# A two-layer graph network on one core: who gathers the source rows, and how many instructions make the messages

## The chip, the cores and the metric

The kernel runs on one NeuronCore of a Trainium2 chip. That core has five engines with instruction queues of their own: TensorE (PE, matrix products, with a weight load PEld that overlaps them), VectorE (DVE), ScalarE (ACT), GpSimd (POOL) and SyncE (SP). SP, ACT and POOL also issue DMA transfers. PE and the transposing and element-wise instructions here meet in PSUM, the accumulators' memory; everything else lies in SBUF. The metric is the device time of one execution in microseconds. A profiled execution gives the busy time of each engine, who waited for whom, and the clock that was granted to PE.

## What is computed

Two message-passing layers over the same graph of 6250 nodes and 200000 edges, each followed by a residual and a layer norm. A node has 160 features: 64 scalars and 32 vectors of three components. Every edge has a source `src`, a target `dst` (sorted), four attributes (one scalar e0, one vector e1) and ten radial features. Cut to what matters:

```python
# layer 0: messages are products of the source row with the edge's attributes
ss, vv = s[src], v[src]
dot  = einsum('eui,ei->eu', vv, e1)
out0 = C0 * (ss * e0 @ W1 + dot * INV3 @ W2)
out1 = C1 * (p3 + p4 + p5)                     # products of ss, vv, e0, e1 with W3, W4, W5
m_agg = segment_sum(concat(out0, out1), dst)
x1 = layernorm(x + (x + relu(m_agg @ Ws_Wv)))

# layer 1: a small network of the radial features weights the source row (the factor node_vec1 of a node is left out here)
h = relu(edge_attr_10 @ W_fc1 / sqrt(10)) * sqrt(2)
w0, w1, w2, w3 = split(h @ W_fc2 / sqrt(100))   # 64, 64, 32, 32 columns
y0, y1 = l0[src], l1[src]                       # rows of x1 @ W_l1
m0 = w0 * y0 * e0
m1 = (w1 * y0)[:, :, None] * e1[:, None, :]
m2 = (w2 * e0)[:, :, None] * y1
m3 = w3 * einsum('eud,ed->eu', y1, e1) * INV3
out = layernorm(x1 + (x1 @ W_si + 0.5 * segment_sums(m0..m3, dst) @ W_l2))
```

## The kernel before

The sorted edges are cut into 391 chunks (`NCH`) of 512 edges; a chunk is four tiles (`J`) of 128 edges. A chunk's targets fall into a narrow window of nodes, at most 32 wide; the first 312 chunks (`HALF`) have one window each, the last 79 have two, one for each half of the partitions. `ORDER` mixes the two kinds, eight of the first and then up to four of the second, and `POS` is a chunk's place in it.

A layer (`sums`, L355) is a software pipeline: a loop over steps t runs a list of stages, each with a lag, on the chunk whose turn it is (L656 to L667). The order of instructions on every engine is the order of that loop, since the schedule is manual.

- `load` gathers the source rows of a chunk, one indirect DMA on POOL for each tile of 128 rows (`gathered`, L245, L247). The table is `x` in layer 0 and `ytab`, the transformed rows, in layer 1. The buffers `g` are a ring of eight chunks (`GRING`), shared by both layers; the first three chunks go to `early` before anything else runs. In layer 1 it also loads the radial features; in both, now and then, the attributes of 32 chunks.
- `onehot` makes, for every edge, its one-hot row in the window, times each of the four attributes (L457, L461, VectorE); `S` is a ring of three.
- In layer 1 `hidden` makes the first part of the radial network: for every second chunk two products into one PSUM tile `ph` (L470), and for every chunk one ReLU on ScalarE into `h` (L473). `message` then does half a chunk at a time: two products into a PSUM tile `pw` of two tiles (L483, two buffers), and three multiplications of the gathered rows with it on VectorE (L486, L491 twice). So a chunk takes six VectorE instructions.
- `matmuls` multiplies the one-hot tiles with the gathered rows (layer 0) or the messages (layer 1), and adds up in a PSUM tile `ab` for each window (L503): four blocks of 32 partitions, one for each attribute.
- `add` transposes 32x32 blocks of `ab` on VectorE into the free columns of the same tile (L524 in layer 1, L526 in layer 0) and adds the result to `acc` at the window's place (L528). In layer 1 the sums of attribute 0 are needed from the first half of the columns, those of the others from the second; `joined` therefore copies attribute 0's block first, 32 partitions by 160 columns, with ScalarE (L510), over the second half, and VectorE transposes that half alone.

When the last chunk that touches a block of 128 nodes is through, the block is closed by a second list of steps: in layer 0 a projection (L547), ReLU, residual, layer norm, a turn (L597), a linear map (L611, L612), and the rows of `ytab` and `btab` are written (L540, L623). Layer 1 cannot gather before all of `ytab` is in DRAM. In layer 1 a block is projected into a part of the tile `bank` (L634), gets its residual (L639) and norm, and is sent. At step 8 (`PREPARE`) of layer 0 the weights are loaded on SP's queue and scaled on VectorE (`prepare`, L286; L350 scales `wc`).

In layer 0 POOL has two helpers. In every run of 16 places (`EVERY`), the fourth tile of two chunks isn't gathered by POOL: the source numbers of that tile are loaded into one partition (L377), and SP (for the last place of the 16) or ScalarE (for the eighth) reads eight of them a step into registers (L395) and starts eight plain row copies (L399) into a tile `row`. When the chunk comes, ScalarE copies `row` to the fourth tile of `g` (`place_rows`, L404). That begins with the chunk at place 15 and holds for 47 chunks.

Of the kernel before, what the change touches and what calls it, by code (L numbers as in the profile page):

```python
# [10 lines left out]
F32 = mybir.dt.float32  # L11
BF16 = mybir.dt.bfloat16
I32 = mybir.dt.int32
AF = mybir.ActivationFunctionType
ALU = mybir.AluOpType
# [33 lines left out]


EVERY = 16
ROWS = P // EVERY
# [68 lines left out]
def gnn_kernel(ctx: ExitStack, tc: tile.TileContext, x, src, dst, ea, sh, avec,  # L121
# [117 lines left out]
    with tc.If(go > 0) as both:  # L239
        windowed(tc, x, srcs, src, rel, low, ident, iota, early, ahead, ea, sh, avec, *weights, out)  # L240
# [4 lines left out]
def gathered(nc, g, srcs, table, c, tiles=J):  # L245
    for j in range(tiles):
# [6 lines left out]
def windowed(ctx: ExitStack, tc: tile.TileContext, x, srcs, src, rel, low, ident, iota, early, ahead, ea, sh, avec,  # L253
# [24 lines left out]
    wn2 = const.tile([M1, 2 * D], F32, name="wn2")  # L278
# [76 lines left out]
    def sums(layer, table, gp, hp):  # L355
        with ExitStack() as s:
# [5 lines left out]
            rp = s.enter_context(tc.tile_pool(name=f"r{layer}", bufs=2))  # L362
            pa = s.enter_context(tc.tile_pool(name=f"pa{layer}", bufs=3 if layer else 4, space=PSUM))
            if layer:
                ph_ = s.enter_context(tc.tile_pool(name="ph", bufs=1, space=PSUM))
                pp = s.enter_context(tc.tile_pool(name="pp", bufs=2, space=PSUM))
            s.enter_context(tc.manual_schedule())
            G, S, SH, ET, H, M, PA, AT, RAW, NUM, ROW = ({} for _ in range(11))


            helpers = {} if layer else {EVERY - 1: (nc.sync, mybir.EngineType.SP),
                                       EVERY // 2 - 1: (nc.scalar, mybir.EngineType.Activation)}
            helped = {ORDER[i] for i in range(EVERY // 2, NCH) if i % EVERY in helpers}

            def numbers(c):
                NUM[c] = rp.tile([1, P], I32, name=f"num{POS[c] % EVERY}")
                nc.sync.dma_start(NUM[c], src[:, c, J - 1:J].rearrange("p a -> a p"))  # L377

            def fetch_rows(c):
                i = POS[c]  # L380
                for place, (queue, engine) in helpers.items():

                    k = (i - place - 1) % EVERY
                    due = i - k + EVERY - 1
                    if due >= NCH or ORDER[due] not in helped:
                        continue
                    d = ORDER[due]
                    if d not in NUM:
                        numbers(d)
                    if d not in ROW:  # L390
                        ROW[d] = rp.tile([P, D], F32, name=f"row{place}")
# [670 lines left out]
```

## Time and profile before

| | |
|---|---|
| median of 14 runs | 3905.62 us (3904.21 to 3907.64) |
| the profiled execution | 3905.87 us |
| its span | 3904.0 us |
| busy: PE / DVE / ACT / POOL | 3077.5 / 2027.8 / 492.0 / 2916.6 us |
| share of the span | 79% / 52% / 13% / 75% |
| mean granted clock of PE | 0.802 |
| moved by DMA | 296.88 MB, 76 GB/s |

The 40 slices of the page, 97.6 us each, show two stages, with the layers' border near the middle of the twentieth:

```profile
PE   3345677777777777766788899899999999999998
...
DVE  4223323333333334344466666666666767777776
ACT  2000000000000000001111111111111111111111
POOL 7777777777777777777577777777777777777776
PEclk7666655555655565667799999999999999999999
```

A digit is the busy share in tenths; PEclk is the granted clock of PE. The groups that follow are costly lines of the page, as line, engine, operation, output and inputs, count, busy time, mean of one in nanoseconds, and the idle time just before them:

```profile
L503 PE MATMUL ab<-m,S 128*128 128x320 f32 (+1 forms) x3760 | 958.5, 445 | 4.4 <-DVE acc L528 3.5
L483 PE MATMUL pw<-fc,h 100*128 100x192 f32 x3128 | 662.0, 343 | 159.4 <-DVE m L491 80.6
...
L486 DVE TENSOR_TENSOR m<-pw,g 128x256 f32<-128x256 f32 x782 | 330.7, 423 | 523.5 <-DMA g<-ytab,srcs 434.0
...
L491 DVE TENSOR_TENSOR m<-g,pw 128x192 f32<-128x192 f32 x1564 | 476.5, 346 | 0.0
...
L510 ACT ACTIVATE ab<-ab 32x160 f32<-32x160 f32 x470 | 121.3, 265 | 1353.5 <-PE ab L503 1138.3
L473 ACT ACTIVATE h<-ph 100x512 f32<-100x512 f32 x391 | 228.3, 584 | 208.1 <-PE ph L470 204.1
...
L524 DVE STREAM_TRANSPOSE ab<-ab 128x160 f32<-128x160 f32 x470 | 167.5, 356 | 13.6 <-issue 8.8
```

PE shows two instructions for each product of this data type. 470 is the number of windows, 1564 that of tiles.

### The profile page before, as it was taken

How to read it: one execution, taken by the hardware profiler on the slowest of the kernel's cores; microseconds unless marked ns; L12 is line 12 of the kernel's file. 1: busy time of each engine (PE TensorE's matmuls, PEld its weight loads, DVE VectorE, ACT ScalarE, POOL GpSimd, SP SyncE). 2: the span in 40 equal slices, each digit the busy share in tenths (PEclk: the TensorE clock that was granted, in tenths of full speed). 3: DMA queues.
4: the chain of work that ended last, by engine and by line, in shares of the span. 5: the costliest groups of instructions: out<-in, count | busy, mean ns of one | idle time of the engine just before them, and what ended most of it. 6: DMA issues, size and time to landing. Idle time of an engine off the chain costs nothing.

```text
span 3904.0 us, 61514 instructions
## 1 busy us (share of the span) xinstructions
PE 3077.5 (79%) x12754; PEld 2112.2 (54%) x12755; DVE 2027.8 (52%) x6485; ACT 492.0 (13%) x1264; POOL 2916.6 (75%) x3086
## 2 busy tenths in 40 slices
PE   3345677777777777766788899899999999999998
PEld 3234444454445555544555566566666666666666
DVE  4223323333333334344466666666666767777776
ACT  2000000000000000001111111111111111111111
POOL 7777777777777777777577777777777777777776
PEclk7666655555655565667799999999999999999999
DMA  3323333333333333333223332333333333333332
GB/s 83 74 69 73 73 76 73 75 74 81 76 77 76 79 77 82 77 82 85 67 73 73 74 74 71 75 74 76 74 80 76 77 77 77 75 81 75 81 77 69
DMA packets 215130, 296.88 MB, mean 76 GB/s; under 512 B 71494, under 2 KB 158156, under 8 KB 214746
## 3 DMA queue, kind: packets, MB, share of 16 engines
q0 software_dynamic: 147888, 252.59, 27.0%
q1 hardware_dynamic: 53782, 33.56, 3.1%
q10 hardware_dynamic: 13076, 6.70, 0.7%
q8 instruction: 107, 1.75, 0.2%
q14 instruction: 277, 2.27, 0.2%
HBM read 280.60 MB, written 12.00 MB: 75 GB/s over the span
## 4 chain that ended last, share of the span: by engine, by line
POOL 23%; issue 21%; DMA 21%; PE 16%; DVE 9%; ACTq 5%; SPq 5%; ACT 1%; DVEq 0%; POOLq 0%
POOL g L247 23%; DMA g<-ytab,srcs 10%; PE ab L503 8%; DMA g<-in_x,srcs 7%; ACTq L399 4%; SPq L399 3%; DVE m L491 3%; DMA row<-in_x 3%; PE pw L483 3%; DVE m L486 2%; PE ph L547 1%; ACTq L395 1%; SPq L395 1%; PE ph L470 1%; DVE ab L524 1%
## 5 line engine op out<-in xcount | busy, mean ns | idle before, releaser
L247 POOL DMA_INDIRECT g<-ytab,srcs x1564 | 1479.5, 946 | 500.1 <-issue 397.6
L247 POOL DMA_INDIRECT g<-in_x,srcs x1505 | 1425.1, 947 | 462.1 <-issue 403.4
L503 PE MATMUL ab<-g,S 128*128 128x160 f32 (+1 forms) x3736 | 1019.0, 459 | 562.9 <-DMA g<-in_x,srcs 298.0
L503 PEld LDWEIGHTS ab<-g,S 128*128 128x128 f32 (+1 forms) x3736 | 695.3, 278 | 893.2 <-DMA g<-in_x,srcs 478.1
L503 PE MATMUL ab<-m,S 128*128 128x320 f32 (+1 forms) x3760 | 958.5, 445 | 4.4 <-DVE acc L528 3.5
L483 PE MATMUL pw<-fc,h 100*128 100x192 f32 x3128 | 662.0, 343 | 159.4 <-DVE m L491 80.6
L483 PEld LDWEIGHTS pw<-fc,h 100*128 100x128 f32 x3128 | 504.1, 191 | 424.5 <-issue 306.5
L503 PEld LDWEIGHTS ab<-m,S 128*128 128x128 f32 (+1 forms) x3760 | 612.4, 193 | 219.8 <-issue 44.4
L486 DVE TENSOR_TENSOR m<-pw,g 128x256 f32<-128x256 f32 x782 | 330.7, 423 | 523.5 <-DMA g<-ytab,srcs 434.0
L526 DVE STREAM_TRANSPOSE ab<-ab 128x160 f32<-128x160 f32 x470 | 169.5, 361 | 647.6 <-PE ab L503 643.4
L491 DVE TENSOR_TENSOR m<-g,pw 128x192 f32<-128x192 f32 x1564 | 476.5, 346 | 0.0
L461 DVE TENSOR_TENSOR S<-bank,sh 128x384 f32<-128x384 f32 (+2 forms) x782 | 431.6, 552 | 61.9 <-PE ab L503 11.7
L528 DVE TENSOR_TENSOR acc<-acc,ab 128x120 f32 (+2 forms) x940 | 261.4, 278 | 216.7 <-ACT acc L584 143.0
L510 ACT ACTIVATE ab<-ab 32x160 f32<-32x160 f32 x470 | 121.3, 265 | 1353.5 <-PE ab L503 1138.3
L473 ACT ACTIVATE h<-ph 100x512 f32<-100x512 f32 x391 | 228.3, 584 | 208.1 <-PE ph L470 204.1
L457 DVE TENSOR_TENSOR bank<-ramp,rel 128x96 f32<-128x96 f32 (+2 forms) x782 | 200.9, 257 | 18.1 <-PE bank L634 17.7
L524 DVE STREAM_TRANSPOSE ab<-ab 128x160 f32<-128x160 f32 x470 | 167.5, 356 | 13.6 <-issue 8.8
L621 DVE SCALAR_TENSOR_TENSOR base<-pl,a_sb,z 128x160 f32<-128x160 f32 (+1 forms) x49 | 18.8, 384 | 281.5 <-ACT y L618 257.0
L547 PE MATMUL ph<-w_or_et,acc 128*128 128x160 f32 (+1 forms) x490 | 130.9, 446 | 5.5 <-DVE acc L528 5.0
L547 PEld LDWEIGHTS ph<-w_or_et,acc 128*128 128x128 f32 (+1 forms) x490 | 122.2, 312 | 15.9 <-issue 6.7
L470 PE MATMUL ph<-early,fc 10*100 10x512 f32 x392 | 110.9, 632 | 2.3 <-DMA early<-in_ea 2.3
L470 PE MATMUL ph<-w_or_et,fc 10*100 10x512 f32 x390 | 109.1, 628 | 3.0 <-DMA w_or_et<-in_ea 2.9
(95 smaller groups left out, 820.1 us busy)
## 6 DMA issues: line engine op xcount, KB each, us to landing
row<-in_x SPq DMA_DIRECT2D x3072, 0.6 KB
row<-in_x ACTq DMA_DIRECT2D x2944, 0.6 KB
g<-ytab,srcs POOLq DMA_INDIRECT x1564
g<-in_x,srcs POOLq DMA_INDIRECT x1505
raw<-in_sh SPq DMA_DIRECT2D x88, 64.0 KB
early<-in_ea SPq DMA_DIRECT2D x98, 40.0 KB
xt<-in_x SPq DMA_DIRECT2D x48, 80.0 KB
ytab<-y ACTq DMA_DIRECT2D x48, 80.0 KB
```

The lines of the kernel that those rows point to most:

```text
L247: nc.gpsimd.indirect_dma_start(out=g[:, j, :], out_offset=None, in_=table, in_offset=bass.IndirectOffsetOnAxis(ap=srcs[:, c, j:j + 1], axi ...
L399: queue.dma_start(ROW[d][a + n:a + n + 1, :], table[ds(at[n], 1), :])
L461: nc.vector.tensor_tensor(S[c][:, :, :, :w], oh[:, :, None, :w].to_broadcast([P, J, 4, w]), attr[:, :, :, None].to_broadcast([P, J, 4, w]) ...
L470: nc.tensor.matmul(ph[:, i, :], fc1[g:g + 10, :], ET[c // 4][g:g + 10, c % 4 // 2, :], start=True, stop=True)
L473: nc.scalar.activation(H[c], H["p"][:, c % 2, :].rearrange("f (p j) -> f j p", j=J), AF.Relu, scale=FC_SCALE)
L483: nc.tensor.matmul(pw[:, j, :], h[:, q + j, :], fc2, start=True, stop=True)
L486: nc.vector.tensor_tensor(mq[:, :, :, 0:64], pw[:, :, 0:128].rearrange("p j (a u) -> p j a u", a=2), y[:, :, None, 0:64].to_broadcast([P, ...
L491: nc.vector.tensor_tensor(mq[:, :, a, 64:160].rearrange("p j (d u) -> p j d u", d=3), y1, pw[:, :, None, w:w + 32].to_broadcast([P, 2, 3, ...
L503: nc.tensor.matmul(ab[:, :n], one[h * i:h * i + h, j, :, :], t[h * i:h * i + h, j, :], start=(j == 0), stop=(j == J - 1), skip_group_check ...
L524: nc.vector.transpose(tr, blocks[:, 1])
L528: nc.vector.tensor_tensor(v, v, tr[:, :, :width(c)], op=ALU.add)
L547: nc.tensor.matmul(po[:r], lhs, weights[:, g, :], start=(g == 0), stop=(g == 4))
```

## The change

The helpers of layer 0 go: `numbers`, `fetch_rows` and `place_rows` with their stages and pools, and `gathered` always takes all four tiles. In layer 1 `hidden` makes one activation for the two chunks that share `ph`. `message` takes a chunk at a time: `pw` becomes one tile of four times 256 columns (192 used) with a single buffer in place of two tiles of two, and each of the three multiplications covers the whole chunk. `joined` goes; `add` transposes the second half of `ab` for all partitions and then the first half for partitions 0 to 31, over the first result. The last residual `z` moves into the space of the weights `wn2`, which layer 1 doesn't use, in two slots by turns.

```diff
@@ -46,10 +46,6 @@
 
 FINAL = NCH - 25
 AHEAD = 3
-EVERY = 16
-ROWS = P // EVERY
 FOLD = 104
 
 
@@ -237,20 +233,20 @@
     go = nc.values_load(fits[0:1, 0:1], min_val=0, max_val=1,
                         skip_runtime_bounds_check_because="a comparison's result")
     with tc.If(go > 0) as both:
-        windowed(tc, x, srcs, src, rel, low, ident, iota, early, ahead, ea, sh, avec, *weights, out)
+        windowed(tc, x, srcs, rel, low, ident, iota, early, ahead, ea, sh, avec, *weights, out)
     with both.Else():
         general(tc, x, srcs, rel, dst, ea, sh, avec, *weights, out)
 
 
-def gathered(nc, g, srcs, table, c, tiles=J):
-    for j in range(tiles):
+def gathered(nc, g, srcs, table, c):
+    for j in range(J):
         nc.gpsimd.indirect_dma_start(out=g[:, j, :], out_offset=None, in_=table,
                                      in_offset=bass.IndirectOffsetOnAxis(ap=srcs[:, c, j:j + 1], axis=0))
     return g
 
 
 @with_exitstack
-def windowed(ctx: ExitStack, tc: tile.TileContext, x, srcs, src, rel, low, ident, iota, early, ahead, ea, sh, avec,
+def windowed(ctx: ExitStack, tc: tile.TileContext, x, srcs, rel, low, ident, iota, early, ahead, ea, sh, avec,
              w1t, w2t, w3t, w4t, w5t, ws, wv, wsi0, wsi1, wl10, wl11,
              w00, w10, w01, w11, wfc1, wfc2, out):
 
@@ -275,7 +271,9 @@
     w_or_et = const.tile([P, 7 * D], F32, name="w_or_et")
     wb = w_or_et[:, :5 * D].rearrange("p (g d) -> p g d", d=D)
     wn = w_or_et[:, 5 * D:]
-    wn2 = const.tile([M1, 2 * D], F32, name="wn2")
+
+    wn2_or_z = const.tile([P, 2 * D], F32, name="wn2_or_z")
+    wn2 = wn2_or_z[:M1]
     wc = const.tile([P, 5, D], F32, name="wc")
     fc1 = const.tile([P, 100], F32, name="fc1")
     fc2 = const.tile([100, 192], F32, name="fc2")
@@ -359,53 +357,16 @@
             if not layer:
                 pn = s.enter_context(tc.tile_pool(name="pn", bufs=1, space=PSUM))
                 up = s.enter_context(tc.tile_pool(name="up", bufs=1))
-            rp = s.enter_context(tc.tile_pool(name=f"r{layer}", bufs=2))
             pa = s.enter_context(tc.tile_pool(name=f"pa{layer}", bufs=3 if layer else 4, space=PSUM))
             if layer:
                 ph_ = s.enter_context(tc.tile_pool(name="ph", bufs=1, space=PSUM))
-                pp = s.enter_context(tc.tile_pool(name="pp", bufs=2, space=PSUM))
+                pp = s.enter_context(tc.tile_pool(name="pp", bufs=1, space=PSUM))
             s.enter_context(tc.manual_schedule())
-            G, S, SH, ET, H, M, PA, AT, RAW, NUM, ROW = ({} for _ in range(11))
-
-
-            helpers = {} if layer else {EVERY - 1: (nc.sync, mybir.EngineType.SP),
-                                       EVERY // 2 - 1: (nc.scalar, mybir.EngineType.Activation)}
-            helped = {ORDER[i] for i in range(EVERY // 2, NCH) if i % EVERY in helpers}
-
-            def numbers(c):
-                NUM[c] = rp.tile([1, P], I32, name=f"num{POS[c] % EVERY}")
-                nc.sync.dma_start(NUM[c], src[:, c, J - 1:J].rearrange("p a -> a p"))
-
-            def fetch_rows(c):
-                i = POS[c]
-                for place, (queue, engine) in helpers.items():
-
-                    k = (i - place - 1) % EVERY
-                    due = i - k + EVERY - 1
-                    if due >= NCH or ORDER[due] not in helped:
-                        continue
-                    d = ORDER[due]
-                    if d not in NUM:
-                        numbers(d)
-                    if d not in ROW:
-                        ROW[d] = rp.tile([P, D], F32, name=f"row{place}")
-                    if k == EVERY // 2 and due + EVERY < NCH:
-                        numbers(ORDER[due + EVERY])
-                    a = k * ROWS
-                    _, at = nc.values_load_multi_w_load_instructions(
-                        NUM[d][0:1, a:a + ROWS], engines=[engine], min_val=0, max_val=N - 1,
-                        skip_runtime_bounds_check_because="node numbers")
-                    for n in range(ROWS):
-                        queue.dma_start(ROW[d][a + n:a + n + 1, :], table[ds(at[n], 1), :])
-
-            def place_rows(c):
-                if c in helped:
-                    del NUM[c]
-                    nc.scalar.activation(G[c][:, J - 1, :], ROW.pop(c), AF.Copy)
+            G, S, SH, ET, H, M, PA, AT, RAW = {}, {}, {}, {}, {}, {}, {}, {}, {}
 
             def load(c):
                 if layer or c not in ahead:
-                    G[c] = gathered(nc, gp.tile([P, J, D], F32, name="g"), srcs, table, c, J - (c in helped))
+                    G[c] = gathered(nc, gp.tile([P, J, D], F32, name="g"), srcs, table, c)
                 else:
                     G[c] = ahead.pop(c)
                 if c % 4 == 0 and layer:
@@ -464,33 +425,35 @@
             def hidden(c):
 
                 if c % 2 == 0:
-                    ph = H["p"] = ph_.tile([100, 2, CH], F32, name="ph")
-                    for i in range(min(2, NCH - c)):
+                    n = min(2, NCH - c)
+                    ph = ph_.tile([100, 2, CH], F32, name="ph")
+                    for i in range(n):
                         g = 64 * i
                         nc.tensor.matmul(ph[:, i, :], fc1[g:g + 10, :], ET[c // 4][g:g + 10, c % 4 // 2, :],
                                          start=True, stop=True)
-                H[c] = wp.tile([100, J, P], F32, name="h")
-                nc.scalar.activation(H[c], H["p"][:, c % 2, :].rearrange("f (p j) -> f j p", j=J),
-                                     AF.Relu, scale=FC_SCALE)
+                    h = wp.tile([100, 2, J, P], F32, name="h")
+                    nc.scalar.activation(h[:, 0:n], ph[:, 0:n, :].rearrange("f i (p j) -> f i j p", j=J),
+                                         AF.Relu, scale=FC_SCALE)
+                    for i in range(n):
+                        H[c + i] = h[:, i]
 
             def message(c):
 
                 m = M[c] = wp.tile([P, J, 320], F32, name="m")
                 h = H.pop(c)
-                for q in range(0, J, 2):
-                    pw = pp.tile([P, 2, 192], F32, name="pw")
-                    for j in range(2):
-                        nc.tensor.matmul(pw[:, j, :], h[:, q + j, :], fc2, start=True, stop=True)
-                    y = G[c][:, q:q + 2, :]
-                    mq = m[:, q:q + 2, :].rearrange("p j (a u) -> p j a u", a=2)
+                pw = pp.tile([P, J, 256], F32, name="pw")
+                for j in range(J):
+                    nc.tensor.matmul(pw[:, j, 0:192], h[:, j, :], fc2, start=True, stop=True)
+                y = G[c]
+                mq = m.rearrange("p j (a u) -> p j a u", a=2)
+                nc.vector.tensor_tensor(
+                    mq[:, :, :, 0:64], pw[:, :, 0:128].rearrange("p j (a u) -> p j a u", a=2),
+                    y[:, :, None, 0:64].to_broadcast([P, J, 2, 64]), op=ALU.mult)
+                y1 = y[:, :, 64:160].rearrange("p j (d u) -> p j d u", d=3)
+                for a, w in ((0, 128), (1, 160)):
                     nc.vector.tensor_tensor(
-                        mq[:, :, :, 0:64], pw[:, :, 0:128].rearrange("p j (a u) -> p j a u", a=2),
-                        y[:, :, None, 0:64].to_broadcast([P, 2, 2, 64]), op=ALU.mult)
-                    y1 = y[:, :, 64:160].rearrange("p j (d u) -> p j d u", d=3)
-                    for a, w in ((0, 128), (1, 160)):
-                        nc.vector.tensor_tensor(
-                            mq[:, :, a, 64:160].rearrange("p j (d u) -> p j d u", d=3), y1,
-                            pw[:, :, None, w:w + 32].to_broadcast([P, 2, 3, 32]), op=ALU.mult)
+                        mq[:, :, a, 64:160].rearrange("p j (d u) -> p j d u", d=3), y1,
+                        pw[:, :, None, w:w + 32].to_broadcast([P, J, 3, 32]), op=ALU.mult)
 
             def matmuls(c):
                 one = S.pop(c)
@@ -504,11 +467,6 @@
                                          start=(j == 0), stop=(j == J - 1), skip_group_check=True)
                 del G[c]
 
-            def joined(c):
-
-                for ab in PA[c]:
-                    nc.scalar.activation(ab[0:32, D:2 * D], ab[0:32, 0:D], AF.Copy)
-
             def add(c):
                 for w, ab in zip(windows(c), PA.pop(c)):
                     if w % 8 == 0:
@@ -521,7 +479,9 @@
                     tr = ab[:, n:].rearrange("p (b f) -> p b f", f=W)
                     blocks = ab[:, :n].rearrange("p (l b f) -> p l b f", b=5, f=32)
                     if layer:
+
                         nc.vector.transpose(tr, blocks[:, 1])
+                        nc.vector.transpose(tr[0:32], blocks[0:32, 0])
                     else:
                         nc.vector.transpose(tr, blocks[:, 0])
                     v = acc[:, :, ds(AT[w // 8][w % 8], width(c))]
@@ -635,7 +595,8 @@
 
             def residual_last(b):
                 r = rows(b)
-                z = T["z", b] = np_.tile([P, D], F32, name="z")
+                turn = sorted(CLOSE, key=CLOSE.get).index(b) % 2
+                z = T["z", b] = wn2_or_z[:, D * turn:D * turn + D]
                 nc.vector.scalar_tensor_tensor(z[:r], T.pop(("po", b))[:r], a_sb[:r, b:b + 1],
                                                T.pop(("base", b))[:r], op0=ALU.mult, op1=ALU.add)
                 moments(b, z)
@@ -645,11 +606,11 @@
                 sent_rows(nc.sync, b, out[b * P:b * P + rows(b), :], T.pop(("o", b)))
 
             if layer:
-                stages = [(load, 0), (joined, 4), (onehot, 1), (hidden, 1), (add, 4), (message, 2), (matmuls, 3)]
+                stages = [(load, 0), (onehot, 1), (hidden, 1), (add, 4), (message, 2), (matmuls, 3)]
                 parts = [(fetch_base, 3, 2), (project_last, 5, 4), (residual_last, 6, 5), (deviation, 7, 5),
                          (sent, 8, 6)]
             else:
-                stages = [(fetch_rows, 0), (load, 0), (place_rows, 1), (onehot, 1), (add, 3), (matmuls, 2)]
+                stages = [(load, 0), (onehot, 1), (add, 3), (matmuls, 2)]
                 parts = [(fetch, 4, 1), (project, 6, 3), (rectify, 6, 4), (residual, 8, 4), (deviation, 9, 4),
                          (lambda b: normed("x1", b), 10, 5), (turned, 11, 5), (kept, 12, 5), (linear, 13, 7),
                          (written, 14, 7)]
```

## The prediction

> **What bounds the kernel now.** First the costliest groups of the page, then the waits of POOL, which say whether that engine ever stands still.
>
> ```profile
> L247 POOL DMA_INDIRECT g<-ytab,srcs x1564 | 1479.5, 946 | 500.1 <-issue 397.6
> L247 POOL DMA_INDIRECT g<-in_x,srcs x1505 | 1425.1, 947 | 462.1 <-issue 403.4
> ...
> POOL g L247 <- issue: 800.9, 2628, 0.3
> POOL g L247 <- PE ab L503: 49.9, 153, 3.6
> ...
> POOL g L247 <- DMA btab<-base: 23.9, 1, 23.9
> ```
>
> The share of POOL is only 75%, but the idle time is made of 0.3 us pieces: one between every two gathers, whatever the releaser is called. A gather takes 0.946 us, then 0.30 us pass, then the next one starts. Only two waits are longer, 3.6 us and 23.9 us. The timeline gives the ends of the two chains of gathers:
>
> ```profile
> 19.95 0.95 POOL L247 DMA_INDIRECT g<-in_x,srcs  x1 [0.30 <-issue]
> ...
> 1905.98 0.95 POOL L247 DMA_INDIRECT g<-in_x,srcs  x1 [0.30 <-issue]
> ...
> 1930.86 0.94 POOL L247 DMA_INDIRECT g<-ytab,srcs  x1 [23.93 <-DMA btab<-base]
> ...
> 3885.57 0.95 POOL L247 DMA_INDIRECT g<-ytab,srcs  x1 [0.30 <-issue]
> ```
>
> Layer 1: (3885.57 - 1930.86) / 1563 = 1.2506 us from one gather to the next, so both layers hang on POOL from end to end. Layer 0, without its 3.27 us of extra wait: (1905.98 - 19.95 - 3.27) / 1504 = 1.2518 us. The profiled span is thus 20.0 us of start, 1886 us of layer 0 gathers, 24.9 us of turn, 1954.7 us of layer 1 gathers and 18.4 us of end; 1.87 us lie outside it (3905.87 - 3904.0). The 14 runs have a median of 3905.62, 0.25 below this execution.
>
> The next view is the windows of the whole core. It shows the room that the other engines have:
>
> ```profile
> 1000.00:1500.00 500.00, 376.92 (x1232) 248.42 (x1232) 186.75 (x547) 35.08 (x107) 378.06 (x400) 0.59 0.32 78
> ...
> 3000.00:3500.00 500.00, 463.06 (x2118) 318.62 (x2115) 356.82 (x1120) 90.48 (x236) 378.36 (x400) 0.99 0.31 77
> ```
>
> The columns are PE, PEld, DVE, ACT and POOL busy, granted clock, DMA share and GB/s. Each has exactly 400 gathers in 500 us. In layer 1 a chunk (four gathers, 5.00 us) holds 463.06/100 = 4.63 us of PE, 3.57 us of DVE, 0.90 us of ACT. So PE has 0.37 us a chunk to spare, and that is where the change could do harm.
>
> **The gathers given back to POOL.** The two helpers fetch one tile of 128 rows each in every 16 chunks: 3072 + 2944 rows are 47 tiles (47 placing activations at L404). The order of the changed program on POOL is 12 + 1552 + 1564 gathers instead of 12 + 1505 + 1564, so 47 more, all in layer 0: 47 x 1.2506 = **+58.8 us**. Nothing hides them. All 3128 gathers together need 3128 x 1.2506 = 3912 us, more than the whole time now. What goes with the helpers, 6016 row copies on the queues of SP and ACT at 0.41 us a row, their register loads, 47 index loads and 47 activations of 336 ns, is off that path and is worth nothing by itself, except in two places.
>
> The first is the stall near the start:
>
> ```profile
> 81.95 0.62 DVE L350 TENSOR_SCALAR wc<-wc 128x800 f32<-128x800 f32 x1 [5.38 <-DMA row<-in_x]
> ...
> 84.24 8.04 PE L503 MATMUL ab<-g,S 128*128 128x160 f32 x39 [9.40 <-issue]
> ...
> 86.98 0.95 POOL L247 DMA_INDIRECT g<-in_x,srcs  x1 [3.57 <-PE ab L503]
> ```
>
> The releaser is named after a row, but what L350 reads is `wc`, whose loads stand on SP's queue behind the helper's rows; it is scaled 5.38 us late; VectorE works in order, the one-hot tiles behind that scaling are late, PE stops for 9.4 us, a gathered buffer comes free late and POOL waits 3.57 instead of 0.30. Without the rows, the 23 loads behind the memsets that end at 62.6 need some 10.5 us of issue (0.45 us each, their spacing now) and 2 us to land: about 75, before VectorE reaches L350 at 76.57. **-3.3 us**; at worst 0.
>
> The second is the turn between the layers:
>
> ```profile
> 1885.72 3.04 PE L503 MATMUL ab<-g,S 64*128 64x160 f32 x20 [5.19 <-ACT g L404]
> ```
>
> The last helped chunk holds PE until 1885.7, and PE and VectorE carry that backlog to the end: the last chunk's matmuls end near 1912.4, though its last gather ends at 1906.93 and should land about 2.66 us later (as the one at 1008.22 did), so 1910.1 with the last matmuls. **-2.0 us** of the 24.9; between -2.3 and 0.
>
> **Layer 1's messages.** Six instructions a chunk become three of double size. From 423 ns for 256 elements and 346 for 192, 1.2 ns an element and 115 fixed: 512 takes 731, 384 takes 577, so 1.89 us instead of 2.23, -135 us of VectorE over 391 chunks (bounds: nothing, and half of the six, -436). The second transpose adds at most 470 x 0.36 = 167 us (the row of L524), at least 0. VectorE ends near where it was, 3.57 + 0.08 us a chunk of 5.00. On ACT 121 us of copies go, and 391 activations of 584 ns become 196 of about 1.05 (0.9 ns an element from the 160- and 512-element rows). ACT is 18% busy there. All this is worth **0** while POOL's 5.00 us cover it.
>
> What can cost is the buffer of `pw`: one of four tiles in place of two of two. The next chunk's eight `pw` passes now wait for the third message instruction of this chunk, and the message starts when all four tiles have landed, not two. Queued behind them on PE are the scatter matmuls of the chunk, its projection and `ph`; VectorE's message and add wait for these, then the ring of eight gathered buffers, then POOL, which notices after some seven chunks (35 us) of lag. In a loop: after the scatter of chunk c-2 ends, VectorE needs 0.82 (one-hot) + two windows of 0.36 + 0.36 + 0.28 + message 1.89 = 4.71 us, PE 1.57 + 2.4 = 4.0 and in most iterations 1.0 to 1.6 more. Both are under 5.00, except where a block ends (1.4 us of VectorE more, once in eight chunks); the lag drains.
>
> **The end.** There a block closes every second chunk, and the chain of waits stays on PE without a gap:
>
> ```profile
> 3885.42 1.56 PE bank L634 x10
> 3886.98 1.30 PE pw L483 x8
> 3888.28 2.40 PE ab L503 x16
> ```
>
> For the last chunk the whole message stands in place of its second half (+0.77), two transposes are added (+0.71), two waits for ACT's copies go (-0.5), and I allow +0.5 for PE behind the single `pw`. **+1.5 us**; at least -0.9 (copies gone, transposes covered), at most +5.5 (0.4 us in each of the last ten chunks besides).
>
> **Sum.** 3904.0 + 58.8 - 3.3 - 2.0 + 1.5 = 3959.0; with 1.87 outside, **3961 us**, 55 above the median. Lower end: 3904.0 + 58.8 - 3.3 - 2.3 - 0.9, and layer 0's gathers at layer 1's distance (1552 x 0.0012 = -1.9): 3956. Upper end: no stall and no backlog saved, +5.5 at the end: 3970.
>
> **The skill against the rows.** The Trainium skill, "DMA: Bandwidth & Descriptors", section "Issuing engines are not separate DMA queues", says that starting DMAs from several engines saves only the time of the starting, usually small beside the transfer. By that, giving 47 tiles back to POOL would cost about nothing, and the sum would be 3902. This trace has the other case: the starting, 1.25 us a tile, is what POOL is made of.
>
> **Rivals.** (1) *PE becomes the bound in layer 1.* If the single `pw` leaves half a message (1.1 us before, the part once covered) uncovered on PE in each chunk, 4.63 + 1.1 = 5.73 us against 5.00: 391 x 0.73 = +285, 4246 us; it decides from 0.37 us a chunk. For it: PE's 93%, and 80.6 us of `pw` waits on the message already. Against it: the scatter of the chunk before lies between two groups of `pw`. 6%; most of its cases lie far below that price, from 3970 on.
> (2) *VectorE holds POOL up.* The longest layer 1 gather took 1020 ns, 74 over the median; one such delay for each added transpose is 470 x 0.074 = +35, 3996 us. Against it: the mean is 946 and 947 where VectorE is 37% and 71% busy. 4%.
> The skill's "SBUF — State Buffer", section "SBUF: two separate sides", has the rule that speaks against this change: VectorE in a two-port mode locks GpSimd out while it writes descriptors. If all 470 new transposes did so for their 0.36 us, it would be +169, 4130 us; the 946 and 947 above show nothing of the kind for the transposes already there.
> (3) *Faster: gathers come at a shorter distance once 6016 row copies no longer share the DMA engines.* The place is layer 0; the 1552 gathers there would need 55/1552 = 35 ns less each to break even; at twice that, 1.18 us, it ends at 3906 - 54 = 3852 us. For it: the row of 1.2518 in layer 0 against 1.2506. Against it: that is 1.2 ns, and layer 1, without any row copy, has the same 946 + 300. 3%. That the tiles don't all go to POOL is excluded by the program's order.
>
> **How the numbers follow.** The forecast has 87%, the rivals 6, 4 and 3. The range 3955 to 3970 holds nearly all of the first. A difference under 0.2% (7.8 us) counts as none: slower 0.965, within 0.2% 0.01, faster 0.025.
>
> **What would show it.** In the profile after: 1552 gathers from `in_x`, 1.25 us apart in both layers; no wait of 3.6 us on POOL near 87; first layer 1 gather near 1984 and the last near 3939; some 20 us behind that one. The forecast is wrong if gathers in layer 1 show waits over 0.3 us on the message (rival 1), or last longer than 0.95 (rival 2), or come closer together (rival 3).

## The result and the profile after

| | before | after |
|---|---|---|
| median of the runs | 3905.46 us (28 runs, 3904.17 to 3909.01) | 3963.76 us (6 runs, 3960.45 to 3966.79) |
| ratio | | 1.0148, 95% interval 1.0138 to 1.0158 |
| the profiled execution, and its span | 3905.87 and 3904.0 us | 3965.24 and 3963.5 us |

The changed kernel is 58.3 us slower by the medians and 59.5 us by the spans of the two profiles. The groups of POOL after, then two of its waits (total, times, longest):

```profile
L243 POOL DMA_INDIRECT g<-ytab,srcs x1564 | 1479.7, 946 | 497.9 <-issue 403.3
L243 POOL DMA_INDIRECT g<-in_x,srcs x1552 | 1469.4, 947 | 472.8 <-issue 398.5
...
POOL g L243 <- issue: 801.8, 2632, 0.3
...
POOL g L243 <- DMA ytab<-y: 21.7, 1, 21.7
```

1552 gathers of layer 0 in place of 1505, each as long as before, and behind the first chunks one wait alone that is longer than 0.3 us, the turn between the layers. The timeline of POOL gives the first and the last gather of each layer:

```profile
21.20 0.95 POOL L243 DMA_INDIRECT g<-in_x,srcs  x1 [0.30 <-issue]
...
1962.15 0.95 POOL L243 DMA_INDIRECT g<-in_x,srcs  x1 [0.30 <-issue]
...
1984.80 0.94 POOL L243 DMA_INDIRECT g<-ytab,srcs  x1 [21.70 <-DMA ytab<-y]
...
3939.76 0.94 POOL L243 DMA_INDIRECT g<-ytab,srcs  x1 [0.30 <-issue]
```

Set against the same four points of before, the difference of the spans falls apart like this (us):

| stage | before | after | difference | predicted |
|---|---|---|---|---|
| up to the first gather of layer 0's own chain | 19.95 | 21.20 | +1.25 | 0 |
| layer 0's gathers | 1886.03 | 1940.95 | +54.92 | +58.8 - 3.3 |
| turn | 24.88 | 22.65 | -2.23 | -2.0 |
| layer 1's gathers | 1954.71 | 1954.96 | +0.25 | 0 |
| from the last gather's start to the end | 18.43 | 23.74 | +5.3 | +1.5 |
| sum | 3904.0 | 3963.5 | +59.5 | +55.0 |

The windows of after (start and end, length, then PE, PEld, DVE, ACT and POOL busy, granted clock, DMA share, GB/s) say the same from the other engines' side:

```profile
1000.00:1500.00 500.00, 377.97 (x1177) 245.84 (x1178) 179.71 (x527) 30.38 (x91) 378.17 (x401) 0.58 0.30 74
3000.00:3500.00 500.00, 454.94 (x2088) 319.33 (x2086) 369.93 (x926) 55.29 (x65) 378.39 (x400) 0.98 0.31 77
```

400 gathers in 500 us, as before. ACT has 35 us less to do in the second window, DVE 13 us more, PE 8 us less, and none of it moves the time. What layer 1's edits did to the instructions stands in the groups of VectorE and ScalarE:

```profile
L449 DVE TENSOR_TENSOR m<-pw,g 128x512 f32<-128x512 f32 x391 | 270.5, 692 | 436.8 <-DMA g<-ytab,srcs 389.8
...
L454 DVE TENSOR_TENSOR m<-g,pw 128x384 f32<-128x384 f32 x782 | 394.5, 546 | 0.0
...
L484 DVE STREAM_TRANSPOSE ab<-ab 32x160 f32<-32x160 f32 x470 | 165.4, 352 | 16.2
...
L435 ACT ACTIVATE h<-ph 100x1024 f32<-100x1024 f32 x196 | 200.3, 1022 | 1619.9 <-PE ph L432 1616.1
```

By these rows the three message instructions are busy for 270.5 + 394.5 = 665.0 us; the six half ones were for 330.7 + 476.5 = 807.2. Two instructions in a row overlap at their border, though, and rows of different lines count that twice: taken together, VectorE's instructions that write `m` are busy for 632.2 us, and were for 739.7, so 107 us less. The second transpose costs 352 ns, although it handles a quarter of the partitions of the first (356 ns): 165 us more. VectorE thus has more to do than before, 2106.9 us in the whole instead of 2027.8.

### The profile page after: what moved, and what is told of

Same layout as the page of the kernel before. It is cut to its first block, busy times and chain, and to the rows that moved or that the text cites. A ratio compares the mean times of both kernels' runs of the same rounds, so it can differ in the third digit from the quotient of the medians.

```text
span 3963.5 us, 40347 instructions
## 1 busy us (share of the span) xinstructions
PE 3213.2 (81%) x12754; PEld 2157.6 (54%) x12755; DVE 2106.9 (53%) x5782; ACT 342.0 (9%) x552; POOL 2961.4 (75%) x3133
## 4 chain that ended last, share of the span: by engine, by line
POOL 30%; issue 22%; DMA 22%; PE 15%; DVE 10%; ACT 1%; DVEq 0%; ACTq 0%; POOLq 0%
POOL g L243 30%; DMA g<-in_x,srcs 13%; DMA g<-ytab,srcs 9%; PE ab L466 8%; DVE m L454 3%; DVE m L449 2%; PE ph L507 2%; PE pw L446 2%; DVE S L422 2%; DVE ab L483 1%; PE pl L572 1%; DVE ab L484 1%; PE pl L571 1%; ACT acc L282 1%; DVE bank L418 1%
## 5 line engine op out<-in xcount | busy, mean ns | idle before, releaser
L243 POOL DMA_INDIRECT g<-in_x,srcs x1552 | 1469.4, 947 | 472.8 <-issue 398.5
L466 PE MATMUL ab<-g,S 128*128 128x160 f32 (+1 forms) x3736 | 1173.9, 493 | 508.4 <-DMA g<-in_x,srcs 398.7
L466 PEld LDWEIGHTS ab<-g,S 128*128 128x128 f32 (+1 forms) x3736 | 726.6, 288 | 965.1 <-DMA g<-in_x,srcs 675.3
L446 PE MATMUL pw<-fc,h 100*128 100x192 f32 x3128 | 613.1, 340 | 196.8 <-DVE m L454 96.9
L449 DVE TENSOR_TENSOR m<-pw,g 128x512 f32<-128x512 f32 x391 | 270.5, 692 | 436.8 <-DMA g<-ytab,srcs 389.8
L454 DVE TENSOR_TENSOR m<-g,pw 128x384 f32<-128x384 f32 x782 | 394.5, 546 | 0.0
L435 ACT ACTIVATE h<-ph 100x1024 f32<-100x1024 f32 x196 | 200.3, 1022 | 1619.9 <-PE ph L432 1616.1
L484 DVE STREAM_TRANSPOSE ab<-ab 32x160 f32<-32x160 f32 x470 | 165.4, 352 | 16.2
L543 ACT ACTIVATE rl<-ph 128x160 f32<-128x160 f32 (+1 forms) x49 | 14.9, 304 | 931.6 <-PE ph L507 931.0
```

The source lines that it names most:

```text
L243: nc.gpsimd.indirect_dma_start(out=g[:, j, :], out_offset=None, in_=table, in_offset=bass.IndirectOffsetOnAxis(ap=srcs[:, c, j:j + 1], axi ...
L446: nc.tensor.matmul(pw[:, j, 0:192], h[:, j, :], fc2, start=True, stop=True)
L449: nc.vector.tensor_tensor(mq[:, :, :, 0:64], pw[:, :, 0:128].rearrange("p j (a u) -> p j a u", a=2), y[:, :, None, 0:64].to_broadcast([P, ...
L454: nc.vector.tensor_tensor(mq[:, :, a, 64:160].rearrange("p j (d u) -> p j d u", d=3), y1, pw[:, :, None, w:w + 32].to_broadcast([P, J, 3, ...
L466: nc.tensor.matmul(ab[:, :n], one[h * i:h * i + h, j, :, :], t[h * i:h * i + h, j, :], start=(j == 0), stop=(j == J - 1), skip_group_check ...
L484: nc.vector.transpose(tr[0:32], blocks[0:32, 0])
```

## The experiments

Four chips took part, one for each round of kernels, and on three of them the kernel before itself took 5543 to 5585 us instead of 3905; on the fourth it took 3914.6. Each ratio below is against the kernel before on the same chip, with its 95% interval in brackets, and the first three rounds test the change under another condition than that of the result. No chip was used in two rounds, and the chip of the result is not on record, so the chip and the hour can't be told apart.

**First round (kernel before: 5585.03 us): the parts one by one.** Without the helpers, nothing else changed:

```diff
-            helpers = {} if layer else {EVERY - 1: (nc.sync, mybir.EngineType.SP),
-                                       EVERY // 2 - 1: (nc.scalar, mybir.EngineType.Activation)}
+            helpers = {}
```

> The kernel before, with the two helpers of layer 0 taken out and nothing else. Theory (POOL's chain of gathers is the bound): 47 x 1.2506 = +58.8, no stall near 87 us (-3.3), a shorter turn between the layers (-2.2), the end as before: 3905.5 + 53.3 = 3958.8, that is 5 below the changed kernel; 1552 gathers from in_x 1.25 us apart, about 18.4 us from the last gather's start to the end. Rival (layer 1's edits cost nothing, the longer end of the changed kernel's profile is scatter): 3963.8, the same as the changed kernel.

Measured: 4853.72 us, ratio 0.8688 (0.8668 to 0.8708). Not slower, as the prediction has it where the kernel before takes 3905 us, but 731 us faster.

The changed kernel with the helpers put back, so that only layer 1's edits are left:

```diff
-                stages = [(load, 0), (onehot, 1), (add, 3), (matmuls, 2)]
+                stages = [(fetch_rows, 0), (load, 0), (place_rows, 1), (onehot, 1), (add, 3), (matmuls, 2)]
```

> The changed kernel with the two helpers of layer 0 put back, so that only the edits of layer 1 differ from the kernel before. Theory: layer 1's gathers stay 1.25 us apart and only the end grows, by 3 to 5 us: 3908.5 to 3910.5. Rival (PE or VectorE become the bound behind the single pw buffer): waits of POOL over 0.3 us in layer 1 and well over 3912. Rival (the edits cost nothing): 3905.5.

Measured: 5577.97 us, 0.9989 (0.9971 to 1.0008): no difference.

Of these edits the message, `pw` and the shared activation alone, with `joined` kept:

```diff
-                    pw = pp.tile([P, 2, 192], F32, name="pw")
+                pw = pp.tile([P, J, 256], F32, name="pw")
...
-                H[c] = wp.tile([100, J, P], F32, name="h")
+                    h = wp.tile([100, 2, J, P], F32, name="h")
```

> The kernel before with the whole-chunk message, the single pw buffer and the shared activation, but with ScalarE's copy of attribute 0's sums kept. Of the end's growth by some 3 to 5 us, theory gives this part the whole message for the last chunk (0.77) and PE's waits behind the single buffer (0.5 to 3): 3906.5 to 3909. If the transposes are what costs, 3905.5.

Measured: 5573.96 us, 0.9984 (0.9970 to 0.9999). And the second transpose alone, in place of ScalarE's copy:

```diff
                         nc.vector.transpose(tr, blocks[:, 1])
+                        nc.vector.transpose(tr[0:32], blocks[0:32, 0])
...
-                stages = [(load, 0), (joined, 4), (onehot, 1), (hidden, 1), (add, 4), (message, 2), (matmuls, 3)]
+                stages = [(load, 0), (onehot, 1), (hidden, 1), (add, 4), (message, 2), (matmuls, 3)]
```

> The kernel before with the second transpose on VectorE in place of ScalarE's copy, and nothing else. Theory: two windows of the last chunk, each one transpose more (2 x 0.36) and one wait for a copy less (2 x 0.25): +0.2 at the very end, and up to +1 for PE waiting on VectorE's adds before: 3905.5 to 3907. If the transposes are what costs, 3908.5 or more.

Measured: 5622.72 us, 1.0060 (1.0037 to 1.0083), 38 us more. Its gathers take 949 ns where the other three kernels have 946 or 947, which is some 9 us of it (3069 x 3 ns). The two halves don't add up to the 0.9989 of both together (0.9984 x 1.0060 = 1.0044); why, stays open.

On this chip POOL doesn't set the pace. A gather still takes 0.946 us when it runs, and half of the distances are still 1.25 us, but with the pauses the mean distance is 1.61 us in layer 1, 1.95 in layer 0 with the helpers and 1.43 without them. In layer 1 PE begins a chunk's first `pw` product some 40 us after the chunk's last gather has ended (median, in each kernel of this round), not far from the seven further chunks (7 x 6.4 = 45 us) that the ring lets POOL go ahead: there POOL waits for free buffers. So layer 1's edits had no cover of POOL here, and brought nothing even so.

**Second round (5545.95 us): the first two again, on another chip.**

> The same kernel as e1_helpers_out once more. There the kernel before took 5585 us instead of 3905, and all engines showed pauses of 8 to 9 us that its first profile doesn't have. If that belongs to the chip or its state then, and this chip is like the first one: 3905.5 + 58.8 - 3.3 - 2.2 = 3958.8, 53 above the kernel before beside it. If the pauses are here too: about 0.87 of the kernel before.

Measured: 4829.07 us, 0.8718 (0.8694 to 0.8742).

> The same kernel as e2_layer1_only once more. On a chip like the first one: theory 3908.5 to 3910.5 (only the end grows, layer 1's gathers 1.25 us apart), rival (the edits cost nothing) 3905.5, rival (PE or VectorE become the bound) well over 3912. If the pauses are here too: 0.999 of the kernel before, as in the first run.

Measured: 5535.31 us, 0.9984 (0.9968 to 1.0000). So it was not one odd chip.

**Third round (5543.10 us): what about the helpers costs so much there.** First the changed kernel itself:

> The changed kernel itself, so that it is compared with the kernel before under the condition of this study. Theory A (POOL's gathers are the bound and nothing else is): the ratio on record, 1.0148, whatever the kernel before takes here. Theory B (where the kernel before takes some 5580 us, the instructions of each engine are held up in bursts, and what a kernel pays follows the instructions that its engines must get through in layer 0): what the run without helpers (0.8688) and the run with the layer-1 edits alone (0.9989) give together, 0.868, some 4845 us. If the kernel before takes about 3905 us in this call, both expect 1.0148.

Measured: 4820.66 us, 0.8708 (0.8687 to 0.8728), as theory B had it. Here the change on record makes the kernel 13% faster, and all of that comes from the helpers (0.8718 x 0.9984 = 0.8704).

Then helpers that work as before, but for nothing: POOL gathers all tiles, and no one reads the rows.

```diff
-                    G[c] = gathered(nc, gp.tile([P, J, D], F32, name="g"), srcs, table, c, J - (c in helped))
+                    G[c] = gathered(nc, gp.tile([P, J, D], F32, name="g"), srcs, table, c)
...
-                    nc.scalar.activation(G[c][:, J - 1, :], ROW.pop(c), AF.Copy)
+                    del ROW[c]
```

> The kernel before, whose helpers do all the row copies that they did, but POOL gathers every tile, and nobody waits for the rows (47 copies into g on ScalarE are left out). Theory A: 47 gathers more and no other cost, +55 us, ratio 1.014. Theory B1 (the instructions of SP and ScalarE hold up the whole program, used or not): as the kernel before, 0.98 to 1.02. Theory B2 (they hold up only those who wait for the rows, PE at g): as the run without helpers, 0.86 to 0.90. If the kernel before takes about 3905 us in this call: +55 us by A, B1 and B2 alike.

Measured: 5602.73 us, 1.0111 (1.0085 to 1.0136): B1. It is not waiting for late rows that costs 13%, but the copying itself. POOL's costliest wait there names PE, and VectorE waits for residuals (`xt`), whose loads stand in SP's queue between the row copies (4.5 us in the trace of before):

```profile
POOL g L247 <- PE ab L503: 888.9, 97, 112.8
...
DVE z L589 <- DMA xt<-in_x: 303.9, 30, 17.6
```

And the helper on SP alone:

```diff
-            helpers = {} if layer else {EVERY - 1: (nc.sync, mybir.EngineType.SP),
-                                       EVERY // 2 - 1: (nc.scalar, mybir.EngineType.Activation)}
+            helpers = {} if layer else {EVERY - 1: (nc.sync, mybir.EngineType.SP)}
```

> The kernel before with the helper on SP alone: 24 chunks of layer 0 have their fourth tile copied row by row, 23 go back to POOL. Theory A: 23 gathers more, 23 x 1.2506 = +28.8 us, ratio 1.0074. Theory B with a cost that follows the total of instructions: half of the step of 0.131 that the run without helpers made, 0.93 to 0.94. Theory B with SP's own issue as the bound of layer 0: no gain, 0.98 to 1.01. If the kernel before takes about 3905 us in this call: +28.8 us, less up to 3.3 us if the stall near 87 us goes with the ScalarE helper rather than with SP's.

Measured: 5567.89 us, 1.0049 (1.0031 to 1.0068). Half of the copies cost as much as all of them, which speaks against a price by the total of instructions. Layer 0's gathers span 2938 us with the SP helper alone, 2942 with both (first round), 2977 with idle ones, 2222 without any (first round). The timeline of SP's queue (start, length, copies in it) in the kernel with the SP helper alone:

```profile
1003.05 24.92 SPq L398 DMA_DIRECT2D row<-in_x  x48
...
1029.35 57.88 SPq L398 DMA_DIRECT2D row<-in_x  x32
```

That is 0.52 us a copy in the one stretch and 1.81 in the other. The same view of before, in the profile of the result, has 37 copies in 19.81 us, 0.54 each. From SP's first to its last row copy it is 2949 us here and 1861 us there (the expectations of the fourth round have 2936, for 3052 of the 3072 copies). That made theory C: SP's in-order queue, which also carries the attributes, residuals and weights, is what bounds layer 0 there.

The traces at hand support it. Pauses of over 0.7 us ahead of an instruction of SP that has something to wait for add up to 129 of these 2949 us, and to 98 of 2990 with the idle helpers: SP works through its own instructions nearly without a stop, so a layer that needs them all can't be much shorter. In the trace of before the pauses are 55 of 1862 us, so the queue is almost full even where POOL is the bound; with half of the helper's chunks (fourth round) they are 940 of 1837.

**Fourth round (3914.63 us).** It was to test theory C, but fell on the chip on which the kernel before takes 3914.6 us, so what these kernels tell apart is the prediction's own sum. Gathers take 949 ns on this chip, and the distance in layer 1 is 1.2533 to 1.2537 us against 1.2506: over some 3070 distances 9 us, which is how far the kernel before is from 3905.5.

The helper on ScalarE alone:

```diff
-            helpers = {} if layer else {EVERY - 1: (nc.sync, mybir.EngineType.SP),
-                                       EVERY // 2 - 1: (nc.scalar, mybir.EngineType.Activation)}
+            helpers = {} if layer else {EVERY // 2 - 1: (nc.scalar, mybir.EngineType.Activation)}
```

> The kernel before with the helper on ScalarE alone: 23 chunks of layer 0 helped, 24 back to POOL, SP without row copies. Theory C (where the kernel before takes some 5560 us, SP's own queue is the bound of layer 0: with one helper on it 3052 row copies at 0.962 us are 2936 us of a layer of 2954): without SP's copies layer 0 falls to the 2230 us of the runs without helpers, unless ScalarE's 2944 copies at their 0.948 us (2791 us) bound it in the same way. So C with SP alone held up: ratio 0.87 to 0.89; C with either queue held up: 0.96 to 0.99. Theory B (cost by the total of instructions): 0.93 to 0.94, which the run with one helper on SP (1.0049) already speaks against. If the kernel before takes about 3905 us in this call: 24 x 1.2506 = +30 us, less up to 3.3 us.

Measured: 3943.92 us, +29.3, 1.0075 (1.0058 to 1.0092), for 24 gathers more. POOL's wait near 87 us is gone with SP's rows, but another one stands in the timeline, when the first row of ScalarE's helper comes late:

```profile
165.68 0.95 POOL L247 DMA_INDIRECT g<-in_x,srcs  x1 [6.24 <-PE ab L502]
```

The helper on SP alone, for every other of its chunks:

```diff
-            helped = {ORDER[i] for i in range(EVERY // 2, NCH) if i % EVERY in helpers}
+            helpers = {} if layer else {EVERY - 1: (nc.sync, mybir.EngineType.SP)}
+            helped = {ORDER[i] for i in range(EVERY // 2, NCH) if i % EVERY in helpers and i % (2 * EVERY) < EVERY}
...
```

> The helper on SP alone, and for every other of its chunks: 12 chunks of layer 0 helped, 1536 row copies, 35 gathers back to POOL. Theory C: 1536 x 0.962 = 1478 us are less than the 2230 us that layer 0 takes without helpers, so SP is no longer the bound and the ratio is 0.87 to 0.88, a step of 0.13 for half of the copies. Theory B (each row copy has its price): half way between 1.0049 and 0.87, 0.93 to 0.94. If the kernel before takes about 3905 us in this call: 35 x 1.2506 = +44 us, ratio 1.011.

Measured: 3955.02 us, +40.4, 1.0106 (1.0089 to 1.0123), for 35 gathers more. POOL's wait near 87 us is 1.47 us there.

Both helpers with fixed rows, hence without register instructions; the sums of 47 tiles are those of other nodes:

```diff
-                    _, at = nc.values_load_multi_w_load_instructions(
-                        NUM[d][0:1, a:a + ROWS], engines=[engine], min_val=0, max_val=N - 1,
-                        skip_runtime_bounds_check_because="node numbers")
...
-                        queue.dma_start(ROW[d][a + n:a + n + 1, :], table[ds(at[n], 1), :])
+                        queue.dma_start(ROW[d][a + n:a + n + 1, :], table[a + n:a + n + 1, :])
```

> The kernel before with both helpers, whose 6016 row copies read fixed rows of the table (row a + n), so that no register is loaded or computed: it leaves out the indirection of 47 tiles, and their sums are those of other nodes. SP then issues 3072 copies and no register instructions. If those are what is held up, SP's copies take 0.41 us or less each (1260 us), layer 0 is bound by what bounds it without helpers (2230 us, less 47 gathers), and the ratio is 0.86 to 0.88; if the issue of a copy itself is held up, or both, the copies stay near 0.7 to 0.96 us and the ratio is 0.90 to 1.0. If the kernel before takes about 3905 us in this call: no change (POOL is the bound and gathers as before), 0.998 to 1.002.

Measured: 3909.44 us, -5.2, 0.9986 (0.9976 to 0.9995), inside what was expected. All 6016 copies are still there, POOL's 3081 gathers as well; only SP and ScalarE are through with a copy sooner (0.37 us from one to the next in the median, 0.40 to 0.41 before). Its timeline at the scaling of the weights, and at the turn:

```profile
75.10 0.62 DVE L350 TENSOR_SCALAR wc<-wc 128x800 f32<-128x800 f32 x1 [6.78 <-DMA wc<-in_w]
...
77.28 11.38 PE L500 MATMUL ab<-g,S 128*128 128x160 f32 x62 [12.66 <-issue]
...
1927.91 0.95 POOL L247 DMA_INDIRECT g<-ytab,srcs  x1 [20.45 <-DMA btab<-base]
```

`wc` is scaled at 75.10 and not 81.95, PE goes on at 77.28 and not 84.24, and POOL has no wait over 0.3 us between there and the turn, whose wait is 20.45 and not 23.93 us.

No kernel of the study was faster than the kernel before on this chip and computed the whole of it; where the kernel before takes some 5550 us, the changed kernel and the one without helpers are the fastest (0.8708, and 0.8688 and 0.8718).

## Why the prediction was right

**POOL is the bound, 1.2506 us a gather, +58.8.** Right, and shown at three doses: 47, 24 and 35 gathers given back cost 58.3, 29.3 and 40.4 us by the medians, 1.24, 1.22 and 1.15 us each with all that goes along. In after's trace layer 0 grows by 54.92: 47 x 1.2506 = 58.8, less the stall of 3.3, less 0.6 because the other distances are 1.2514 and not 1.2518 us.

**The stall near 87 us, -3.3.** Right, its cause too. PE goes on 6.7 us earlier than before. One detail was not so: the weights are there near 75, as estimated, but VectorE comes to the scaling 6.12 us earlier than that, and not later. The row names the attributes (`raw`), which are issued next on the same queue; what L348 reads is `wc`. The timeline of after:

```profile
75.51 0.58 DVE L348 TENSOR_SCALAR wc<-wc 128x800 f32<-128x800 f32 x1 [6.12 <-DMA raw<-in_sh]
...
77.55 12.22 PE L466 MATMUL ab<-g,S 128*128 128x160 f32 x66 [12.53 <-issue]
```

The fourth round has the dose: no row copies on SP, no wait there; half of them, 1.47 us; all of them, but issued sooner, none. So it was SP's queue ahead of the weights.

**The turn, -2.0.** Right in size (-2.23). Its reason, the last helped chunk's late rows, is supported by the kernel with fixed rows: that chunk is helped there too, but the 5.19 us in which PE waits for its rows before are gone, and the turn is 21.40 us. It was not tried by itself, and no profile of the kernel before was taken on that chip.

**Layer 1's edits, 0 under POOL's cover.** Right: +0.25 us over 1564 gathers. The estimates of its instructions came out a little high: 731 ns, measured 692; 577, measured 546; 1050, measured 1022; at most 360, measured 352. VectorE has 3.70 us a chunk (predicted 3.65), PE 4.55 of 5.00. What the edits are worth once POOL is no cover is known only from the chips of the first two rounds, where it is nothing for both together (0.9989 and 0.9984).

**The end, +1.5.** Within its bounds (-0.9 to +5.5), but mis-sized: +5.3. The chain that ended last, in after (start, length, what):

```profile
3943.72 1.32 PE pw L446 x8
...
3948.65 1.90 PE ab L466 x12
...
3952.67 1.62 PE bank L594 x10
...
3955.90 0.36 DVE wn_or_z L526
```

The term that was too small is "+0.5 for PE behind the single `pw`": the last `pw` starts 3.01 us after the last gather's end (3940.71), before it was 0.46 (3886.98 after 3886.52), so 2.55. From there to the end of the last normalisation it is 12.54 against 12.01 us, +0.5, where 0.77 + 0.71 - 0.5 = 1.0 had been put. The last 2.2 us, the way of the output to DRAM (7.24 against 5.04 us), were not in the sum.

The 2.55 belong to layer 1's edits. Over all 391 chunks the first `pw` product starts in the median 1.22 us before the chunk's last gather ends; in before it is 3.12, and 3.14 to 3.16 in the three kernels of the fourth round, which have layer 1 as before. So PE runs some 1.9 us later all through layer 1, where POOL covers it, and at the last chunk nothing does: there the product starts, by the timeline, 2.85 us after the gather's end, against 0.31 in before and 0.27, -1.06 and -0.98 in those three. That it is the single buffer, and not another of these edits, was not tried by itself under this condition.

For the rest of the 5.3 it isn't settled: the three kernels take 18.7, 18.7 and 22.8 us from the last gather's start to the span's end, against 18.4 before and 23.7 after. In the one with 22.8 (fixed rows), the chain names a late landing and a slow product:

```profile
3887.36 3.97 DMA g<-ytab,srcs
...
3899.44 3.01 PE bank L631 x10
```

So ends of one and the same layer 1 lie 4 us apart, and that the end came out within its bounds says little.

**The start.** The +1.25 was not foreseen either. It is POOL's very first wait, for the source numbers of the first chunks: 5.03 us in after, 4.03 in before. It is no scatter. Three programs were profiled twice, in different rounds or in the result and a round, and the first gather of layer 0's own chain starts at 21.20 and 21.22 (the changed kernel), 21.17 and 21.22 (without helpers), 19.97 and 19.92 us (layer 1's edits alone). Of all profiles, the seven in which rows of ScalarE's helper are used start it between 19.92 and 20.66, the seven others between 21.17 and 21.23. What in the program moves it stays open.

**The total.** By the spans of the profiles the sum is 4.5 us short (55.0 against 59.5), by the medians 3.3. The forecast holds because the 58.8 of the gathers are right and the rest is small beside them, not because each small term is right: the start was missing, and the end was 3.8 short.

**The rivals.** (1) and (2) did not come: no gather of layer 1 waits more than 0.3 us, and they last 946 ns. Nor is there any sign of the lock of which the Trainium skill tells in "SBUF — State Buffer", section "SBUF: two separate sides", and which the prediction put at 4130 us if every new transpose took it: with 470 transposes more, a gather of layer 1 takes 946 ns as before. (3) did not come either: 1.2514 us between gathers without a single row copy. The rule of the Trainium skill, "DMA: Bandwidth & Descriptors", section "Issuing engines are not separate DMA queues", has the time of starting a DMA as usually small; with that, the prediction came to 3902 us. Measured were 3963.76, since here the starting is the bottleneck.

**Where it would have been wrong.** On the chips of the first three rounds the same edit has the other sign. The step that fails there is "off that path and is worth nothing by itself", said of the 6016 row copies: helpers whose rows nobody reads cost the whole 13%. What makes SP's instructions, PE and VectorE slower there was not found. That SP's queue is the bound of layer 0 (theory C) fits the one helper that costs as much as two and SP's few waits in those traces, but it is not shown by an experiment: the kernels that were to test it ran on a chip where the effect isn't there.

## What to carry to other kernels

When one engine starts a transfer every 1.25 us from the first microsecond to the last, count its starts: here 47 starts were 58.8 us, and all else that the change did on four engines came to less than 1 us in sum (59.5 of the spans less 58.8), savings and losses of 6 to 7 us each. A helper that takes starts off that engine is worth their number times their distance, less what its own queue delays, and the second part is found by asking what else stands in that in-order queue. A helper made of thousands of small instructions is also the part whose price changed most, from a gain of 1.5% to a loss of 13%, between these rounds; measure on more than one chip before it is kept or thrown out.

## What the runs showed of the hardware

The same program took 3905 us in the runs of the result (which chip that was is not on record), 3915 on the chip of the fourth round, and 5543, 5546 and 5585 us on the three others, while single instructions lasted as long as ever (gathers 946 to 950 ns). What differs in the traces there is the time between instructions. On SP, where a register instruction follows another one, 615 of 3051 pairs stood more than 250 ns apart in the kernel with only layer 1's edits, half of them by 714 ns or more, and often several in a row; 444 of the 615 lie within 30 ns of 0.70 or 1.40 us. In the trace of before it was 23 of 3051, all near 384 ns and all a multiple of 128 instructions apart. PE, too, stood still longer: 192 gaps of over 4 us, against 23. Waits of POOL over 4 us fill 29% of that kernel's layer 0, but only 9% of the time of SP's pauses of over 0.6 us lie in them, so most of the pauses fall into times in which POOL does not stand still for long. Slower transfers are not the reason: a packet of the gathers' queue takes 110 ns in that trace and 114 in that of before, one that loads instructions 1098 and 413 ns (on the two queues) and 1124 and 425 before. What makes the pauses, and whether they cause the longer times or only go with them, the runs don't tell.
